# Cross attention of layer 0: weights transposed in blocks of 128 columns across the heads, values spread to fit

## The chip, the core and the metric

The kernel runs on one core of a Trainium2 chip. The core has five instruction queues that run side by side and meet at semaphores: TensorE for matrix products (PE in the profile, with its weight loads shown apart as PEld), VectorE (DVE), ScalarE (ACT), GpSimd (POOL) and SyncE (SP), which here only issues transfers. A queue runs its instructions in the order in which they were written: one that waits holds up all those behind it. The metric is the time of one execution on the device in microseconds; a result is the median over several runs.

## The reference, cut to what matters

The model is a two-layer decoder over x of shape [16, 256, 256], all in float32. Layer 0 has a linear attention, a cross attention to a context of 77 keys, and a mixture of 16 experts with two chosen per token; layer 1 has attention, a second cross attention and a quantized feed-forward block. The change touches the cross attention of layer 0 alone:

```python
q = jnp.einsum('bfd,dnh->bfnh', query_input, wq)      # 16 heads of 16
k = jnp.einsum('btd,dnh->btnh', source_input, wk)     # t: 77 keys
v = jnp.einsum('btd,dnh->btnh', source_input, wv)
q = q * HEAD_DIM ** (-0.5)
logits = jnp.einsum('btnh,bfnh->bnft', k, q) + bias
weights = jax.nn.softmax(logits, axis=-1)
attn = jnp.einsum('bnft,btnh->bfnh', weights, v)
return jnp.einsum('bfnh,nhd->bfd', attn, wo)
```

For each of the 16 batch entries and each of the 16 heads, 256 queries are weighted over 77 keys.

## The kernel before

The 4096 tokens are 32 tiles of 128 (`NT`), four tiles to a group (`NG` = 8), so that a group spans two batch entries. Each of the two stages that matter, `l0_attention` and `l0_cross`, is recorded whole before any of it is issued: `Plan` collects the operations, each with the tiles that it reads and writes, gives each a duration by fixed formulas (`Call`, L308), and then puts them in an order, always taking next the operation that can start first, or one that can start at most 150 ns later and stands earlier in the record. A copy (`nc.copy`, L112) may go to VectorE or to ScalarE, and the planner chooses. Because of the recorder, nearly all instructions of these stages carry the line L363, and the profile has to be read by the names of tiles.

`l0_cross` (L1009) walks over the tiles i = 0 to 31. For tile i it records the scores of tile i+1 ahead of the second half of tile i:

- `scores` (L1032): per half m of the heads (`KD` = 2 halves of 8 heads) two matmuls give `ps_sc`, 128 queries by 8 x 77 keys. VectorE adds the mask (`lx_s`), takes the maximum (`lx_mx`), GpSimd subtracts it, ScalarE takes the exponential, VectorE sums (`lx_sum`) and inverts (`lx_rec`), GpSimd widens the inverse (`lx_wide`).
- `weighted` (L1071): the weights `lx_s` [128 queries, 8 heads, 77 keys] are transposed to have the keys on the partitions. This is done head by head: eight transposes of 77 columns per half, four into each `ps_pt`, and two copies per half to `lx_sT` (77 x 512). Then 16 products `ps_rec` per tile multiply them with the values: each takes the 77 rows of one head and writes 32 rows, for a pair of heads, and two products (`par` 0 and 1) add up in the same place. That works since the values `lx_v` lie in a buffer [77, 16, 4, 16] of which the slots 1 and 2 stay zero, so that each head adds zeros to its neighbour's rows. ScalarE or VectorE copies the transposed inverse (`lx_rT`), VectorE multiplies (`lx_aT`), two products with `w_L_xattn_wo` follow in the same `ps_rec`, and VectorE adds the result to x.
- `cross_keys` (L943) and `cross_queries` (L981) prepare the group after the next: projections of keys, values and queries. The values of group g+2 go by one copy from `ps_v` into one of three `lx_v` buffers. The mask of the group is loaded by SyncE (`lx_bias`).
- the router of the experts (`l0_router`, L773): SyncE first fills `moe_x` with zeros (16 transfers of 640 KB), then, a group behind the attention, 64 scatters from GpSimd (`moe_x<-rh,slot`) write the token rows into it.

The groups 0 and 1 of keys, values and queries are prepared at the end of `l0_attention`, by `ahead` (L735).

The line that places the values before, and the loop of transposes:

```python
    nc.copy(
        X.vz[g % 3][:, :, ::3, :],
        ps[:S2].rearrange("p b (r h e) -> p (b r) h e", h=2, e=DH0),
    )
```

Of the kernel before, what the change touches and what calls it, by code (L numbers as in the profile page):

```python
# [18 lines left out]
F32 = mybir.dt.float32  # L19
# [8 lines left out]
P = 128  # L28
B, S, D = 16, 256, 256
S2 = 77  # L30
NT = B * S // P
NG = NT // 4
KD = D // P
H0 = 16
DH0 = 16
# [446 lines left out]
def matmul_k(E, ps, lhs, rhs):  # L482

    last = len(lhs) - 1
    for n, (a, b) in enumerate(zip(lhs, rhs, strict=True)):
        E.nc.tensor.matmul(ps, a, b, start=n == 0, stop=n == last)  # L486
# [33 lines left out]
def l0_attention(E, W, X, own):  # L520
# [9 lines left out]
    with ExitStack() as ctx, planned(E) as nc:  # L530
        c1 = ctx.enter_context(tc.tile_pool(name="la_c", bufs=1))
        wk = nc.ring(ctx.enter_context(tc.tile_pool(name="la_w", bufs=2)), 2)
        w3 = nc.ring(ctx.enter_context(tc.tile_pool(name="la_w3", bufs=3)), 3)
        pp = nc.ring(ctx.enter_context(tc.tile_pool(name="la_pp", bufs=2, space=PSUM)), 2)
# [194 lines left out]
        f = front(0)  # L729
# [3 lines left out]
        f = front(1)  # L733
        step(f)
        def ahead():  # L735

            cross_consts(E, W, X, own)
            yield
            for g in range(2):
                yield from cross_keys(E, W, X, g, own, pp)  # L740
                yield from cross_queries(E, W, X, g, wk, own, pp)

        for i in range(NT):
# [3 lines left out]
            if i == NT - 4:  # L747
                f = ahead()
# [12 lines left out]
            if a == 3:  # L761
                step(f)
                if i + 5 < NT:
                    f = front(i // 4 + 2)
# [156 lines left out]
def cross_consts(E, W, X, pool):  # L921

    nc = E.nc

    quarter = pool.tile([P, 2, 4], F32, name="lx_quarter")
    nc.gpsimd.memset(quarter, 1.0)
    nc.gpsimd.affine_select(
        quarter, quarter, [[-64, 2], [-16, 4]], ALU.is_ge, 0.0, base=0, channel_multiplier=1
    )
    nc.gpsimd.affine_select(  # L930
        quarter, quarter, [[64, 2], [16, 4]], ALU.is_ge, 0.0, base=15, channel_multiplier=-1
    )
    X.sel = pool.tile([P, 4], F32, name="lx_sel")
    nc.vector.tensor_tensor(X.sel, quarter[:, 0, :], quarter[:, 1, :], ALU.add)

    X.vz = [pool.tile([S2, 16, 4, DH0], F32, name=f"lx_v{n}") for n in range(2)]
    for t in X.vz:
        nc.gpsimd.memset(t, 0.0)  # L940


def cross_keys(E, W, X, g, own, pp):  # L943

    nc = E.nc
    cols = slice(2 * g * S2, (2 * g + 2) * S2)
    kd = []
    for m in range(KD):
        ps = pp.tile([P, 512], F32, name="ps_k", tag="pp")
        matmul_k(  # L950
            E, ps[:, : 2 * S2], [W.xk0[:, k, m * P : (m + 1) * P] for k in range(KD)],
            [W.ctxT[:, k, cols] for k in range(KD)],
        )
        src = ps[:, : 2 * S2].rearrange("p (b k) -> p b k", b=2)

        t = own.tile([P, 2, 4, S2], F32, name=f"lx_k{m}", tag=f"lx_k{m}")
        for n in range(4):
            if n % 2:
                nc.vector.tensor_scalar(
                    t[:, :, n, :], src, X.sel[:, n : n + 1], None, ALU.mult  # L960
                )
            else:
                nc.scalar.activation(t[:, :, n, :], src, AF.Copy, scale=X.sel[:, n : n + 1])
        kd.append(t)
    X.keyed[g] = kd
    yield
    ps = pp.tile([P, 2, D], F32, name="ps_v", tag="pp")
    for j in range(2):
        b = 2 * g + j
        matmul_k(  # L970
            E, ps[:S2, j, :], [W.ctxT[:, k, b * S2 : (b + 1) * S2] for k in range(KD)],
            [W.xv0[:, k, :] for k in range(KD)],
        )
    nc.copy(
        X.vz[g % 3][:, :, ::3, :],
        ps[:S2].rearrange("p b (r h e) -> p (b r) h e", h=2, e=DH0),
    )
    yield


# [28 lines left out]
def l0_cross(E, W, X, raw, made):  # L1009
# [9 lines left out]
    with ExitStack() as ctx, planned(E) as nc:  # L1019
        c1 = ctx.enter_context(tc.tile_pool(name="lx_c", bufs=1))  # L1020
        wk = nc.ring(ctx.enter_context(tc.tile_pool(name="lx_w", bufs=2)), 2)
        w3 = nc.ring(ctx.enter_context(tc.tile_pool(name="lx_w3", bufs=3)), 3)
        pp = nc.ring(ctx.enter_context(tc.tile_pool(name="lx_pp", bufs=3, space=PSUM)), 3)
        psc = nc.ring(ctx.enter_context(tc.tile_pool(name="lx_sc", bufs=2, space=PSUM)), 2)
        pm = nc.ring(ctx.enter_context(tc.tile_pool(name="lx_pm", bufs=1, space=PSUM)), 1)

        third = c1.tile([S2, 16, 4, DH0], F32, name="lx_v2")
        nc.gpsimd.memset(third, 0.0)
        X.vz.append(third)
        R = l0_router(E, W, c1, wk, w3, pp)  # L1030
# [40 lines left out]
        def weighted(i, held):  # L1071

            weights, wide = held
            vb = X.vz[i // 4 % 3]
            r0 = 8 * (i % 4 // 2)
            sT = {}
            for m in range(KD):
                for par in range(2):
                    pt = pp.tile([P, 512], F32, name="ps_pt", tag="pp")
                    for j in range(4):  # L1080
                        nc.tensor.transpose(
                            pt[:S2, j * P : (j + 1) * P], weights[m][:, 2 * j + par, :], E.ident
                        )
                    t = w3.tile([S2, 4, P], F32, name="lx_sT", tag="lx_sT", bufs=4)
                    nc.copy(t.rearrange("p n q -> p (n q)"), pt[:S2])
                    sT[m, par] = t
                yield


            pr = pm.tile([P, 512], F32, name="ps_rec", tag="pm")  # L1090
            for m in range(KD):
                nc.tensor.transpose(
                    pr[:, D + m * P : D + (m + 1) * P],
                    wide[:, 8 * m : 8 * m + 8, :].rearrange("p h e -> p (h e)"), E.ident,
                )
            with nc.together():
                for m in range(KD):
                    for par in range(2):
                        for j in range(4):
                            nc.tensor.matmul(  # L1100
                                pr[32 * j : 32 * j + 32, m * P : (m + 1) * P],
                                vb[:, r0 + 4 * m + j, 2 * par : 2 * par + 2, :].rearrange(
                                    "p r e -> p (r e)"
                                ),
                                sT[m, par][:, j, :], start=par == 0, stop=par == 1,
                                skip_group_check=True,
                            )
            rT = w3.tile([P, D], F32, name="lx_rT", tag="lx_rT", bufs=2)
            nc.copy(rT, pr[:, D:])
            aT = w3.tile([P, D], F32, name="lx_aT", tag="lx_aT", bufs=2)  # L1110
            nc.vector.tensor_tensor(aT, pr[:, :D], rT, ALU.mult)
            yield
            matmul_k(
                E, pr[:, D:], [aT[:, m * P : (m + 1) * P] for m in range(KD)],
                [W.xo0[:, m, :] for m in range(KD)],
            )
            nc.vector.tensor_tensor(E.xs[i], E.xs[i], pr[:, D:], ALU.add)
            yield

        none = iter(())  # L1120

        def step(side, n=1):
            for _ in range(n):
                next(side, None)

        held = scores(0)
        f = kv = route = last = none
        for i in range(NT):
            g, a = divmod(i, 4)
            mine = weighted(i, held)  # L1130
            if a == 0:
                step(route, 8)
                route = R.take(4 * g - 4) if g else none
                kv = cross_keys(E, W, X, g + 2, wk, pp) if g + 2 < NG else none
            if i + 1 < NT:
                held = scores(i + 1)
                mark = len(nc.ops) - 1
            if a == 1 or a == 2:
                step(f)
            step(route, 1 if g < NG - 1 else 3)  # L1140
            step(mine)
            if a == 0:
                step(f)
            else:
                step(kv)
            step(mine)
            step(route, 1 if g < NG - 1 else 3)
            step(mine)
            if a == 3 and i + 5 < NT:
                f = cross_queries(E, W, X, i // 4 + 2, wk, wk, pp)  # L1150
                step(f)
            step(mine)
            if g == NG - 1 and a:

                with nc.urgent(-80):
                    step(route, 8)
                    step(last, 8)
                    last = R.take(i - 1, 2) if a == 1 else R.take(i, 1, 0)
                    step(last, 3)
# [934 lines left out]
```

## Time and profile before

| | |
|---|---|
| median of 16 runs | 1738.24 us (1731.48 to 1742.69) |
| the profiled execution, its time | 1736.84 us |
| its span, first to last instruction | 1735.1 us |
| PE busy in the span | 1590.2 us (92%) |
| DVE busy | 1128.1 us (65%) |
| ACT busy | 733.7 us (42%) |
| POOL busy | 497.8 us (29%) |
| cross attention of layer 0, first scores to first product of the next stage's weights | from about 275 us to about 598 us |
| lx_s transposes, PE | 512 |
| copies ps_pt to lx_sT | 113 on ACT, 15 on DVE |
| ps_rec products with the values | 1024 passes (two for each of 512 products) |

The shares are averages over stages with different limits, so the stage of the change has to be read by itself. A piece that is listed as "x8" is a run of eight instructions in a row; the duration given there is that of the whole run. Matmuls are pipelined: eight transposes of `lx_s` in a row took 1.05 us (from 368.32 us on), while the mean of a single one is listed with 294 ns.

### The profile page before, as it was taken

What the parts mean: (1) busy time and instruction counts of PE and PEld (TensorE: products, weight loads), DVE (VectorE), ACT (ScalarE), POOL (GpSimd) and SP (SyncE); (2) the same over time, 40 slices, a digit from 0 to 9 for tenths busy, and PEclk for the clock granted to TensorE, in tenths of its full rate; (3) what the DMA queues carried; (4) which work ended last, traced back from release to release, by engine and by line L of the source; (5) the groups of instructions that cost most, each with busy time, mean ns of one, the idle gap of its engine ahead of it and who ended that gap; (6) DMA issues with size and microseconds to landing.
All of it is one profiled execution on the core that took longest, in us unless ns stands there. A gap on an engine that the chain in (4) does not pass through costs nothing.

```text
span 1735.1 us, 24227 instructions
## 1 busy us (share of the span) xinstructions
PE 1590.2 (92%) x9268; PEld 1067.3 (62%) x9268; DVE 1128.1 (65%) x2212; ACT 733.7 (42%) x1551; POOL 497.8 (29%) x570
## 2 busy tenths in 40 slices
PE   6999999999996789999997899999999789999799
PEld 3666666666664667777775665666666434433387
DVE  7988876999986343221123778866776643899941
ACT  4343324555553211111112555555555342667850
POOL 5332113565565300000003787433344100000000
PEclk9999999999997599999998999999999889999899
DMA  6000008110001154334322121000000000001111
GB/s 186 1 1 1 2 1 261 62 41 30 29 33 36 53 164 136 109 119 142 122 82 67 43 61 43 13 1 1 1 1 1 1 1 0 25 25 60 37 49 49
DMA packets 75231, 90.76 MB, mean 52 GB/s; under 512 B 11934, under 2 KB 64886, under 8 KB 75114
## 3 DMA queue, kind: packets, MB, share of 16 engines
q1 hardware_dynamic: 68970, 72.64, 13.1%
q0 software_dynamic: 6144, 16.57, 3.0%
q8 instruction: 73, 1.20, 0.3%
q14 instruction: 44, 0.36, 0.1%
HBM read 52.70 MB, written 36.70 MB: 52 GB/s over the span
## 4 chain that ended last, share of the span: by engine, by line
PE 65%; DVE 21%; issue 6%; ACT 4%; DMA 2%; POOL 1%; SPq 1%; another core or an unknown queue 0%; POOLq 0%; ACTq 0%; DVEq 0%
PE ps_y L363 7%; PE ps_h L363 7%; PE ps_pr L363 7%; PE ps_av L363 6%; PE ps_pt L363 5%; PE ps_sc L363 5%; PE ps_out L486 5%; PE ps_gate L486 5%; PE ps_rec L363 3%; PE ps_v L363 3%; PE ps_po L363 2%; DVE ff_g L1957 2%; DVE ff_ps L1828 2%; PE ps_ht L363 2%; DVE ff_pu L1828 1%
## 5 line engine op out<-in xcount | busy, mean ns | idle before, releaser
L363 DVE COPY ex_y<-ps_y 128x256 f32<-128x256 f32 x80 | 33.7, 424 | 217.1 <-PE ps_y L363 217.1
L363 POOL DMA_INDIRECT ex_yg<-moe_y,slot x64 | 63.1, 985 | 346.5 <-issue 345.0
L363 POOL TENSOR_TENSOR sa_e<-sa_e,sa_rec 128x1024 f32<-128x1024 f32 x64 | 121.7, 1908 | 127.4 <-PE ps_pt L363 68.9
L486 PE MATMUL ps_up<-ff_x,ffn_up 128*128 128x512 f32 x336 | 148.7, 601 | 7.1 <-DVE ff_pu L1828 4.3
L363 ACT ACTIVATE sa_e<-ps_sc,sa_top 128x256 f32<-128x256 f32 x256 | 118.0, 484 | 73.1 <-DVE sa_top L363 66.9
L363 PE MATMUL ps_y<-w,ex_h 128*128 128x256 f32 x640 | 141.5, 379 | 5.1 <-DVE ex_y L363 5.1
L363 PE MATMUL ps_h<-ex_xT,w 128*128 128x320 f32 x512 | 142.5, 436 | 0.5 <-ACT ex_h L363 0.5
L363 PEld LDWEIGHTS ps_y<-w,ex_h 128*128 128x128 f32 x640 | 121.4, 190 | 24.4 <-DVE ex_y L363 6.3
L363 ACT ACTIVATE ex_h<-ps_h 128x640 f32<-128x640 f32 x64 | 44.9, 703 | 187.0 <-PE ps_h L363 187.0
L363 PEld LDWEIGHTS ps_h<-ex_xT,w 128*128 128x128 f32 x512 | 96.0, 191 | 40.0 <-ACT ex_h L363 1.0
L486 PEld LDWEIGHTS ps_up<-ff_x,ffn_up 128*128 128x128 f32 x336 | 63.6, 192 | 92.1 <-issue 74.5
L486 PE MATMUL ps_out<-ffn_down,ff_g 128*128 128x256 f32 x384 | 85.9, 388 | 10.3 <-issue 10.3
L486 PE MATMUL ps_gate<-ff_x,ffn_gate 128*128 128x512 f32 x192 | 84.3, 602 | 6.7 <-DVE ff_x L1930 6.7
L486 PEld LDWEIGHTS ps_out<-ffn_down,ff_g 128*128 128x128 f32 x384 | 74.8, 195 | 21.8 <-issue 11.1
L363 DVE TENSOR_REDUCE sa_top<-ps_sc 128x4 f32<-128x1024 f32 x64 | 76.4, 1215 | 16.6 <-PE ps_sc L363 15.1
L363 POOL TENSOR_TENSOR lx_s<-lx_s,lx_mx 128x616 f32<-128x616 f32 x64 | 78.0, 1220 | 31.8 <-DVE lx_mx L363 24.7
L363 DVE TENSOR_TENSOR la_at<-ps_sc,la_tri 128x1024 f32<-128x1024 f32 x64 | 75.8, 1214 | 8.6 <-PE ps_sc L363 8.6
L363 PE MATMUL ps_pt<-ident,lx_s 128*77 128x128 f32 x512 | 77.2, 294 | 0.4 <-ACT lx_sT L363 0.3
L363 ACT COPY lx_sT<-ps_pt 77x512 f32<-77x512 f32 x113 | 61.8, 582 | 28.6 <-PE ps_pt L363 26.5
L363 POOL DMA_INDIRECT moe_x<-rh,slot x64 | 64.2, 1004 | 32.6 <-issue 12.4
L363 PE MATMUL ps_pt<-ident,sa_e 128*128 128x128 f32 x512 | 66.2, 279 | 7.3 <-DVE hT L363 2.3
L363 PEld LDWEIGHTS ps_pt<-ident,lx_s 128*77 128x77 f32 x512 | 63.7, 159 | 12.5 <-issue 5.1
(289 smaller groups left out, 3387.8 us busy)
## 6 DMA issues: line engine op xcount, KB each, us to landing
w<-in_L_ffn_w SPq DMA_DIRECT2D x32, 512.0 KB, 3.8
moe_x<-rt_zero SPq DMA_DIRECT2D x16, 640.0 KB, 8.7
ex_xg<-moe_x SPq DMA_DIRECT2D x15, 640.0 KB, 6.5
moe_y<-ex_y SPq DMA_DIRECT2D x15, 640.0 KB, 5.7
x<-in_x SPq DMA_DIRECT2D x32, 128.0 KB, 3.1
out_x<-x SPq DMA_DIRECT2D x32, 128.0 KB, 1.7
ff_u<-ff_c SPq DMA_DIRECT2D x6, 512.0 KB, 2.9
ff_c<-ff_u SPq DMA_DIRECT2D x6, 512.0 KB, 3.2
```

The source lines that it names most:

```text
L363: made = getattr(getattr(self.nc, self.engine), self.method)(*self.args, **self.kwargs)
L486: E.nc.tensor.matmul(ps, a, b, start=n == 0, stop=n == last)
L1828: E.nc.vector.tensor_reduce(out, in_, axis, ALU.max, apply_absolute_value=True)
L1957: nc.vector.scalar_tensor_tensor(gp, low16(gq, I16), sg16, low16(sig, U16), ALU.mult, ALU.mult)
```

## The change

The weights of one half are taken as one row of 8 x 77 = 616 columns and transposed in blocks of 128 columns, four whole ones and one of 104, without regard to where a head begins. Five transposes replace eight in each half, ten replace 16 in each tile. The four whole blocks of a half fill one `ps_pt` and one `lx_sT` [128, 4, 128]; the two blocks of 104, one from each half, share a third `ps_pt` and a new small tile `lx_sL`.

A pair of heads now lies on two neighbouring blocks: pair j (columns 154j to 154j+153) on the blocks j and j+1. So there are again 16 products per tile, two for each pair, but each over the 128 (or 104) rows of a block, with rows of other pairs meeting zeros. The values must lie accordingly: in a buffer `VALUES` = [128, 4 pairs, 2 parts, 2 batch entries, 2 halves, 32], where the 77 rows of a head stand at the partitions that its columns have in the block. For that the values are first copied to a buffer `lx_vs` (in the ring of `hT`), and 12 transfers per group, issued by SyncE, carry the 8 heads' rows from there into place; four of the eight heads cross a border between blocks and need two.

```diff
-    X.vz = [pool.tile([S2, 16, 4, DH0], F32, name=f"lx_v{n}") for n in range(2)]
+    X.vz = [pool.tile(VALUES, F32, name=f"lx_v{n}") for n in range(2)]
...
+VALUES = [P, 4, 2, 2, KD, 2 * DH0]
+BLOCKS = [(b, min(P, 8 * S2 - b * P)) for b in range(5)]
...
-def cross_keys(E, W, X, g, own, pp):
+def cross_keys(E, W, X, g, wk, own, pp):
...
-    nc.copy(
-        X.vz[g % 3][:, :, ::3, :],
-        ps[:S2].rearrange("p b (r h e) -> p (b r) h e", h=2, e=DH0),
-    )
+    v = wk.tile([P, KD, 512], F32, name="lx_vs", tag="hT")[:S2, 0, :]
+    nc.copy(v, ps[:S2].rearrange("p b d -> p (b d)"))
+    v = v.rearrange("p (b m h e) -> p b m h e", b=2, m=KD, e=DH0)
+    for h in range(8):
+        for b, rows in BLOCKS:
+            lo, hi = max(h * S2, b * P), min((h + 1) * S2, b * P + rows)
+            if lo < hi:
+                nc.sync.dma_start(
+                    X.vz[g % 3][
+                        lo - b * P : hi - b * P, h // 2, b - h // 2, :, :,
+                        h % 2 * DH0 : (h % 2 + 1) * DH0,
+                    ],
+                    v[lo - h * S2 : hi - h * S2, :, :, h, :],
+                )
...
-        third = c1.tile([S2, 16, 4, DH0], F32, name="lx_v2")
+        third = c1.tile(VALUES, F32, name="lx_v2")
...
-            r0 = 8 * (i % 4 // 2)
+            b = i % 4 // 2
...
+            def turn(m, blocks, pt, at):
+                flat = weights[m].rearrange("p h k -> p (h k)")
+                for n, (t, rows) in enumerate(blocks):
+                    nc.tensor.transpose(
+                        pt[:rows, (at + n) * P : (at + n + 1) * P],
+                        flat[:, t * P : t * P + rows], E.ident,
+                    )
+
             for m in range(KD):
-                for par in range(2):
+                pt = pp.tile([P, 512], F32, name="ps_pt", tag="pp")
+                turn(m, BLOCKS[:4], pt, 0)
+                t = w3.tile([P, 4, P], F32, name="lx_sT", tag="lx_sT", bufs=4)
+                nc.copy(t.rearrange("p n q -> p (n q)"), pt)
+                for n in range(4):
+                    sT[m, n] = t[:, n, :]
+                if m == 1:
+                    rows = BLOCKS[4][1]
                     pt = pp.tile([P, 512], F32, name="ps_pt", tag="pp")
-                    for j in range(4):
-                        nc.tensor.transpose(
-                            pt[:S2, j * P : (j + 1) * P], weights[m][:, 2 * j + par, :], E.ident
-                        )
-                    t = w3.tile([S2, 4, P], F32, name="lx_sT", tag="lx_sT", bufs=4)
-                    nc.copy(t.rearrange("p n q -> p (n q)"), pt[:S2])
-                    sT[m, par] = t
+                    for k in range(KD):
+                        turn(k, BLOCKS[4:], pt, k)
+                    t = w3.tile([P, KD, P], F32, name="lx_sL", tag="lx_sL", bufs=2)
+                    nc.copy(t[:rows].rearrange("p n q -> p (n q)"), pt[:rows, : KD * P])
+                    for k in range(KD):
+                        sT[k, 4] = t[:rows, k, :]
                 yield
...
-                    for par in range(2):
+                    for part in range(2):
                         for j in range(4):
+                            rows = BLOCKS[j + part][1]
                             nc.tensor.matmul(
                                 pr[32 * j : 32 * j + 32, m * P : (m + 1) * P],
-                                vb[:, r0 + 4 * m + j, 2 * par : 2 * par + 2, :].rearrange(
-                                    "p r e -> p (r e)"
-                                ),
-                                sT[m, par][:, j, :], start=par == 0, stop=par == 1,
-                                skip_group_check=True,
+                                vb[:rows, j, part, b, m, :], sT[m, j + part],
+                                start=part == 0, stop=part == 1, skip_group_check=True,
                             )
```

In `l0_cross` the call becomes `cross_keys(E, W, X, g + 2, wk, wk, pp)`, in `ahead` `cross_keys(E, W, X, g, wk, own, pp)`; nothing else differs.

## The prediction

> **What bounds the kernel now.** I read the busy times by stretch first, since the shares of the page mix stages. The columns: stretch, its length, then PE, PEld, DVE, ACT and POOL busy with counts, the granted clock, the transfers' share, GB/s.
>
> ```profile
> 288.40:315.20 26.80, 24.53 (x265) 18.68 (x263) 26.16 (x58) 17.20 (x34) 12.59 (x14) 1.00 0.83 273
> ...
> 390.10:427.30 37.20, 33.86 (x308) 24.17 (x308) 33.92 (x92) 20.69 (x42) 22.88 (x30) 1.00 0.11 34
> 427.30:464.50 37.20, 33.86 (x308) 24.16 (x308) 33.91 (x92) 20.68 (x42) 22.85 (x30) 1.00 0.11 34
> ...
> 513.00:597.60 84.60, 57.67 (x431) 43.29 (x430) 49.91 (x161) 29.32 (x57) 42.32 (x57) 0.71 0.13 45
> ```
>
> The cross attention has three parts: a start, a steady part in which four tiles take 37.2 us again and again, and from 513 us a tail, where nothing is full and the clock is 0.71. In the steady part two engines stand almost level: PE 33.86 us and DVE 33.92 us of 37.2. Relief of PE alone can therefore bring only what DVE still loses by waiting. So I looked next at what DVE waited for from 288 to 513 us (total, times, longest):
>
> ```profile
> DVE lx_aT L363 <- ACT lx_rT L363: 8.2, 14, 0.9
> DVE rhT L363 <- PE ps_rt L363: 1.2, 2, 0.8
> DVE lx_s L363 <- PE ps_sc L363: 1.1, 5, 0.2
> ```
>
> With two smaller ones (0.8 and 0.5) this is 11.8 us in 224.6 us, nearly all of it for work that comes out of PE. In the same stretch PE waited 15.7 us for DVE's `lx_aT`. Third, the chain of waits in one period (start, duration, piece):
>
> ```profile
> 411.94 1.29 PE ps_pt L363 x8
> ...
> 413.66 0.44 DVE lx_aT L363
> ...
> 436.37 0.58 DVE lx_sT L363
> ...
> 438.09 0.59 DVE lx_sT L363
> ```
>
> From 404.2 to 427 us the chain runs on PE, and DVE comes in for an `lx_aT` at a time; the period's end lies on DVE, with two copies of transposed weights in it. The pieces with `ps_pt` between 402.2 and 439.4 us add up to 0.46+0.87+1.29+0.66+0.33+1.00+0.50 = 5.1 us.
>
> **The change, part by part.** The durations, from the groups by form:
>
> ```profile
> L363 ACT COPY lx_sT<-ps_pt 77x512 f32<-77x512 f32 x113 | 61.8, 582 | 28.6 <-PE ps_pt L363 26.5 <-issue 2.0
> ...
> L363 ACT COPY sa_eT<-ps_pt 128x512 f32<-128x512 f32 x81 | 44.7, 611 | 14.5 <-PE ps_pt L363 11.8 <-PE ps_cs L363 2.0 <-issue 0.5
> ...
> L363 DVE COPY sa_eT<-ps_pt 128x512 f32<-128x512 f32 x47 | 30.0, 676 | 0.5 <-PE ps_pt L363 0.5
> ...
> L363 ACT COPY lx_rT<-ps_rec 128x256 f32<-128x256 f32 x32 | 11.9, 371 | 51.4 <-PE ps_rec L363 24.3 <-PE ps_pt L363 15.5 <-PE ps_sc L363 8.3
> ```
>
> *Transposes.* 16 per tile become 10. Eight of 77 columns in a row took 1.05 us, of which 0.27 is the last one's way through: (1.05-0.27)/7 = 0.111 us each. Sixteen of 128x128 (`sa_e`, layer 1) took 1.91 us: (1.91-0.28)/15 = 0.109. So width costs nothing and number does: 6 x 0.11 = 0.66 us a tile, 2.6 us a period, 21 us over 32 tiles of PE.
>
> *Products with the values.* 16 per tile as before; 32 passes over 77 rows took 1.01 us on the chain, and `ps_av<-la_at,la_v`, 128 rows and the same 32 columns, has a mean of 276 ns against 285. Nothing.
>
> *Copies.* The order in which the two built programs' instructions stand tells what the planner chose. Before: 113 `lx_sT` on ACT and 15 on DVE. After: 58 `lx_sT` and 22 `lx_sL` on ACT, 6 and 10 on DVE; one `lx_vs` and seven instead of three `rhT` go to DVE as well. ACT loses 113 x 0.582 - 58 x 0.611 - 22 x 0.371 = 22 us, and some more with `rhT`. DVE: 10 x 0.42 (256 wide, as its `ex_y` copies, 424 ns) + 6 x 0.676 + 0.67 + 4 x 0.69 = 11.7 us against 15 x 0.669 = 10.0. So DVE gets 1.7 us more in the stage, 0.2 to 0.3 us a period. But in the period that I compared, the two copies at its end are gone, and one of each kind stands in the middle instead.
>
> *What of it lies on the path.* At the most DVE stops waiting: 11.8 - 1.7 = 10.1 us. At the least nothing: PE's time goes into waits for DVE, 15.7 us now and more then. PE's part of the chain shrinks by 24/64 of 5.1 = 1.9 us a period, while DVE can give 11.8/6 = 2.0 less its 0.25, so 1.7; DVE should be the limit, with some waits left, since `lx_aT` still needs the last product, then a copy. I take two thirds, 6.5 us, and keep 0 and 10.1.
>
> *The start.* The first tile's transposes run at half clock (18 in 3.58 us, 0.2 each) on the chain; six fewer give 1.2 us; the copies behind them are fewer too, but the last product now waits for the small one. I take 1 us (0 to 1.2).
>
> *The tail.* On the chain from 515 to 585 us stand 0.89+1.03+0.26+0.90+0.23 us of `ps_pt` at full clock, 3.05 at half, then 4 x 1.81: 13.6 us. Six of sixteen gone would be 5.1 us. Against it: `ps_rec` now waits for the small copy, 0.37 us and the ways around it, in each of four tiles, and between the tiles the chain runs over DVE and POOL, where nothing changes. I take 3 us (-1 to 5.1).
>
> *Transfers.* 12 for each of 8 groups, of four pieces of 64 bytes per partition: 8 x 77 x 32 = 19712 packets. The page's hardware queue has 68970 packets in 13.1% of 16 engines' 1735 us, 53 ns each, at about 1 KB; at that price all of mine are 1.0 ms over 16 engines, 65 us of a stage of 320 us whose transfers fill 0.11 of the time in the steady part. They are covered: the values of group g+2 are written while group g runs, a whole period of 37 us ahead of their use, and a load of comparable smallness, `cx_bq`, landed after 4.3 us. For group 0 the copy was at 252.9 us and the first use at 286.8; twelve issues of 0.5 us and two rounds of 4.3 us end near 268. What SP has behind them: in `ahead` the loads for layer 1 (not used before 597 us), then two masks and the 16 zero fills of `moe_x` (277.9 to 304.3 us). Group 1's twelve come before most of those loads, group 2's among the zeros, where SP also waits for a copy (298.1 us before): 24 x 0.5 = 12 us later, landing by about 304 + 12 + 8.7 = 325 us. The first scatter was issued at 336.3 us; 11 us of cover, and POOL stalls beyond it.
>
> For how a transfer is spread, the Trainium skill (DMA: Bandwidth & Descriptors, Why a DMA increments its semaphore by 16 and not by 1) says that the number of engines is the largest up to 16 that divides the outermost sizes: 77 rows would go over 11 engines, 51 over 3, the single row over one. By that the 51 rows are 68 packets on each of three engines, an estimate of 3.6 us at 53 ns; it would change no term, and no run here shows it yet.
>
> *Sum.* 6.5 + 1 + 3 = 10.5 us off the span of 1735.1, so 1724.6; the profiled execution took 1736.84, 1.7 us around its span, and lies 1.4 us under the median of 1738.24. That makes 1727.7; I say 1728.
>
> **The rivals.** *DVE takes it all* (17%): PE is faster and waits. For it: DVE's 33.9 of 37.2 us and 1.7 us more of work. Against: its waits come from PE. Then the steady part gives 0 to 2, the tail as much: 1735 to 1739, say 1737.
>
> *PE loses its clock* (12%), the case on the slow side. One place in the trace shows it:
>
> ```profile
> 313.00:316.40 3.40, 1.06 (x16) 0.68 (x5) 3.23 (x10) 0.89 (x2) 1.39 (x3) 1.00 0.00 0
> 316.40:320.00 3.60, 3.60 (x15) 2.31 (x14) 2.93 (x6) 2.69 (x5) 2.24 (x3) 0.53 0.00 0
> ```
>
> After a wait of 2.33 us for `lx_aT` the clock was half for some 3.4 us. In the steady part it never was; the emptiest stretches there (374.4 to 377.8) have PE busy 2.43 of 3.40 us. In the new order one tile of each period has its `w_L_xattn_wo` products directly after the 16 products, where two score matmuls stood between, so PE waits there for copy and multiplication without cover, some 1.6 us and more if DVE is late. A half-clocked 3.4 us costs up to 1.7 us. Six such, one in each period, eat 10 us and give no change; two in each cost 20 - 10.5, so 1748. It decides from seven on.
>
> The skill (TensorE: Matmul & The Clock Gate, Why this matters for your kernels) asks for no PE gap over about 3 us. By that rule no gap here would cost the clock and the sum stays; the trace lost it after 2.33 us, and the trace decides.
>
> *Late zeros* (5%): were the fills to land 15 us after the first scatter is due, GpSimd's queue, with the subtractions behind, would stand still that long: 1728 + 15 = 1743.
>
> **How the numbers follow.** The forecast has 66%. Its own range is the sum of the lower bounds, 0+0-1, to that of the upper ones, 10.1+1.2+5.1: 1739 to 1722; the tail's clock (0.71 on the mean, half and full by turns) may shift by two spells of up to 1.7 us either way, so 1718 at the low end. To the high end I add part of the clock's case: 1742. 0.2% is 3.5 us, about what a measurement of this kernel can tell from no change: faster (under 1734.8) is the forecast, 0.66; no change is DVE's case, 0.17; slower is the clock and the zeros, 0.17.
>
> **What would show it.** Right: a period of 35 to 36.5 us; PE near 31.3 us in it, DVE near 34; DVE's waits for `lx_rT` down to some 4 us; no `lx_sT` copies on DVE at the period's end; zeros landed before the first scatter. Wrong: a period of 37 us or more with PE waiting for `lx_aT` over 20 us (DVE's case); spells of half clock between 320 and 513 us (the clock's); POOL waiting for SP's transfers at its first scatter; PE waiting for a transfer at `ps_rec`. A tail no shorter would take 3 us from the forecast.

## The result, and the profile after

The changed kernel takes 1756.07 us (median of 11 runs, 1751.34 to 1763.80) against 1737.66 us for the kernel before (1731.26 to 1742.69). The ratio is 1.0109, 95% interval [1.0096, 1.0122]: slower by 1.1%, some 19 us, where 10 us less were forecast. The profiled execution spans 1754.0 us against 1735.1.

| part of the profiled execution, us | before | after | forecast |
|---|---|---|---|
| first `lx_aT` after | 288.4 | 296.7 (+8.3) | -1 |
| steady part, first to 25th `lx_aT` | 213.2 | 225.2 (+12.0) | -6.5 |
| tail, to the next stage's weights | 95.8 | 94.9 (-0.9) | -3 |
| all behind it | 1137.7 | 1137.3 (-0.4) | 0 |

The busy times by stretch of the kernel after (start and end, length, then PE, PEld, DVE, ACT, POOL busy with counts, granted clock, transfers' share, GB/s); a line is four tiles, the last one the tail:

```profile
323.20:359.50 36.30, 32.37 (x284) 22.42 (x284) 33.09 (x90) 18.28 (x37) 22.10 (x28) 0.95 0.41 127
359.50:404.00 44.50, 36.51 (x288) 23.75 (x288) 37.49 (x97) 18.06 (x36) 24.75 (x32) 0.92 0.13 34
404.00:439.20 35.20, 32.03 (x282) 22.03 (x280) 32.73 (x93) 18.23 (x36) 21.76 (x28) 0.96 0.15 37
...
478.20:521.90 43.70, 33.35 (x284) 22.84 (x284) 35.76 (x96) 18.72 (x37) 25.02 (x32) 0.96 0.14 39
521.90:616.80 94.90, 64.28 (x480) 45.81 (x481) 62.55 (x195) 30.96 (x62) 47.61 (x68) 0.74 0.12 41
```

Before, a period was 37.1 to 37.5 us with 91 to 94 instructions on DVE. Now two are 35.2 and 36.3 us, as forecast, one is 39.0, and two are 44 us; the longest has 97 instructions on DVE, a shorter one 90: the planner's new order no longer repeats. No period has the full clock: seven spells of 3.4 us at half clock fall into the steady part, where there was one, at 316.4 us.

The border first. The waits of the kernel after from 262 to 297 us (total, times, longest), and SP's timeline (start, duration):

```profile
DVE ln_st L363 <- DMA lx_v<-lx_vs: 13.9, 1, 13.9
POOL lx_v L363 <- DMA lx_v<-lx_vs: 13.6, 1, 13.6
```
```profile
254.80 10.44 SPq L363 DMA_DIRECT2D lx_v<-lx_vs  x12
...
271.05 10.24 SPq L363 DMA_DIRECT2D lx_v<-lx_vs  x12
```

Twelve issues take 10.4 us, not 6. Nobody waits there for values: `ln_st` and the clearing of the third `lx_v` are first writes of the new stage that wait until group 1's transfers have read `lx_vs`, and SP issues the last of those at 281 us.

The steady part, the timeline of the kernel after around one stall (the bracket gives the idle time before and what ended it):

```profile
380.97 1.06 POOL L363 DMA_INDIRECT moe_x<-rh,slot  x1 [1.27 <-ACT lx_sT L363]
381.15 10.43 SPq L363 DMA_DIRECT2D lx_v<-lx_vs  x12
...
381.96 0.27 PE L363 MATMUL ps_rec<-lx_sL,lx_v 104*32 104x128 f32 x1
382.16 0.79 PE L363 MATMUL ps_sc<-lx_k,lx_q 64*128 64x308 f32 x4
...
382.88 0.77 PE L363 MATMUL ps_pt<-ident,lx_s 128*128 128x128 f32 x5
...
385.88 0.37 ACT L363 COPY lx_rT<-ps_rec 128x256 f32<-128x256 f32 x1 [4.68 <-remote]
...
386.76 2.07 PE L363 MATMUL ps_rec<-w_L_xattn_wo,lx_aT 128*128 128x256 f32 x4 [3.12 <-DVE lx_aT L363]
```

The last product ended at 382.23 us by its record, but ACT's copy behind it began at 385.88: PE's increment of the semaphore stands in the trace at 385.86, 3.6 us late, and those of the scores and transposes behind it follow within 0.12 us. DVE and then PE wait, and from 386.4 us PE runs at half clock. The same stands at 460.9 and 507.5 us. A semaphore is the counter by which one engine tells another that its work is done; I call this a late increment. "Remote" stands in the view where the profile names no instruction that ended the wait.

The terms of the copies came about as costed (611, 371 and 420 ns), in the groups by form:

```profile
L363 ACT COPY lx_sT<-ps_pt 128x512 f32<-128x512 f32 x58 | 33.6, 585 | 29.3 <-PE ps_pt L363 23.6 <-issue 4.1 <-remote 1.3
...
L363 ACT COPY lx_sL<-ps_pt 104x256 f32<-104x256 f32 x22 | 8.3, 376 | 1.8 <-PE ps_pt L363 1.6
...
L363 DVE COPY lx_sL<-ps_pt 104x256 f32<-104x256 f32 x10 | 4.2, 420 | 2.0 <-PE ps_pt L363 1.8
```

### The profile page after: what moved, and what is told of

It reads as the page before. It is cut to its first block, busy times and chain, and to the rows that moved or that the text cites. A ratio compares the mean times of both kernels' runs of the same rounds, so it can differ in the third digit from the quotient of the medians.

```text
span 1754.0 us, 23970 instructions
## 1 busy us (share of the span) xinstructions
PE 1583.9 (90%) x9076; PEld 1052.2 (60%) x9076; DVE 1130.2 (64%) x2218; ACT 714.2 (41%) x1513; POOL 498.7 (28%) x570
## 4 chain that ended last, share of the span: by engine, by line
PE 59%; DVE 24%; issue 7%; ACT 4%; POOL 3%; DMA 2%; SPq 1%; another core or an unknown queue 0%; POOLq 0%; DVEq 0%; ACTq 0%
PE ps_y L363 7%; PE ps_h L363 7%; PE ps_pr L363 7%; PE ps_av L363 5%; PE ps_out L486 5%; PE ps_gate L486 5%; PE ps_sc L363 4%; PE ps_pt L363 4%; PE ps_v L363 3%; PE ps_po L363 2%; DVE x L363 2%; DVE sa_top L363 2%; DVE ff_g L1985 2%; PE ps_rec L363 2%; DVE ff_ps L1856 2%
## 5 line engine op out<-in xcount | busy, mean ns | idle before, releaser
L486 PE MATMUL ps_out<-ffn_down,ff_g 128*128 128x256 f32 x384 | 85.9, 388 | 10.3 <-issue 10.3
L363 PE MATMUL ps_sc<-sa_latT,sa_q 64*128 64x256 f32 x512 | 69.7, 399 | 2.0 <-ACT sa_e L363 2.0
L363 PEld LDWEIGHTS ps_pt<-ident,sa_e 128*128 128x128 f32 x512 | 58.9, 145 | 18.2 <-DVE hT L363 4.0
L486 PEld LDWEIGHTS ps_gate<-ff_x,ffn_gate 128*128 128x128 f32 x192 | 37.0, 194 | 53.5 <-issue 52.7
```

The source lines that it names most:

```text
L363: made = getattr(getattr(self.nc, self.engine), self.method)(*self.args, **self.kwargs)
```

## The experiments

Chips differ. On two of them the kernel before takes 1721 to 1722 us, on the three others 1737 to 1742. Each of the five was used once, so that it is the chip, and not the occasion, is not shown. Times are therefore compared as ratios to the kernel before on the same chip, and parts within one chip wherever that is possible; which chip the two first profiles come from is not on record. "Late" says whether increments over 1.1 us late stand between 320 and 510 us; "half" is the time at half clock in the steady part.

| run | ratio [95%] | first lx_aT | steady | half | late |
|---|---|---|---|---|---|
| e1_no_transfers | 1.0017 [0.9998, 1.0035] | 288.0 | 221.2 | 20.5 | yes |
| e2_own_source | 1.0061 [1.0040, 1.0082] | 288.3 | 228.6 | 30.7 | yes |
| e3_only_01 | 1.0081 [1.0052, 1.0109] | 296.0 | 221.1 | 20.5 | yes |
| e4_before_plus | 1.0087 [1.0056, 1.0118] | 288.6 | 227.6 | 17.1 | yes |
| e5_six_more | 1.0083 [1.0055, 1.0110] | 288.4 | 214.6 | 3.4 | no |
| e6_later_end | 1.0064 [1.0037, 1.0091] | 287.8 | 210.6 | 10.2 | no |
| e7_border_later | 1.0035 [1.0020, 1.0050] | 289.5 | 210.0 | 10.2 | no |
| e8_no_scatters | 1.0006 [0.9994, 1.0019] | 289.9 | 211.2 | 17.1 | no |
| e9_later_2000 | 1.0079 [1.0064, 1.0094] | 291.4 | 229.7 | 30.7 | yes |
| e10_later_600 | 1.0053 [1.0037, 1.0069] | 288.0 | 223.0 | 21.2 | yes |
| e11_before_later | 1.0056 [1.0043, 1.0069] | 287.8 | 225.8 | 17.1 | yes |
| e12_before | 1.0001 [0.9991, 1.0011] | 288.2 | 212.8 | 0 | yes |
| f1_before | 0.9999 [0.9983, 1.0015] | 287.7 | 206.0 | 3.4 | no |
| f2_no_transfers | 1.0042 [1.0025, 1.0059] | 289.4 | 212.7 | 10.3 | no |
| f3_six_more | 1.0085 [1.0054, 1.0116] | 289.6 | 214.5 | 3.4 | no |
| f4_later_end | 1.0050 [1.0030, 1.0071] | 289.7 | 210.1 | 10.2 | no |
| f5_after | 1.0113 [1.0079, 1.0147] | 296.2 | 228.7 | 23.9 | yes |
| f6_after_no_scatters | 1.0004 [0.9992, 1.0015] | 296.1 | 211.1 | 17.1 | no |

e1 to e4, e5 to e8, e9 to e12, f1 to f4, and f5 with f6 each shared a chip.

### What the transfers cost (e1 to e4)

e1 leaves the transfers out when the planned order is issued, so that the order stays; e3 does it with `drop=g > 1`:

```diff
-                    v[lo - h * S2 : hi - h * S2, :, :, h, :],
+                    v[lo - h * S2 : hi - h * S2, :, :, h, :], drop=True,
...
-        made = getattr(getattr(self.nc, self.engine), self.method)(*self.args, **self.kwargs)
+        made = None if self.drop else getattr(getattr(self.nc, self.engine), self.method)(*self.args, **self.kwargs)
```

> The changed kernel in its own order of instructions, with all 96 transfers that place the values left out (the values stay zero, so the output is not the reference's). Theory A, the transfers cost the time, once at the border between the stages and again in every period: the first lx_aT comes near 288 us again, the steady part to the 25th lx_aT takes 205 to 214 us instead of 225.2, and the time is 1726 to 1732 us. Rival B, the new order of the products costs it by way of the clock: the border's 8 us come back and no more, the steady part stays at 222 to 226 us with its spells of half clock, and the time is near 1748 us.

> The changed kernel in its own order, with the transfers of the groups 0 and 1 kept and those of groups 2 to 7 left out (their values are then those of earlier groups or zero). Theory A: the border stays late by 8 us (first lx_aT near 297 us), the steady part takes 205 to 214 us, the time is 1734 to 1741 us. Rival B: steady part 222 to 226 us, the time stays at 1754 to 1758 us.

Ratios 1.0017 without any and 1.0081 with those of the groups 0 and 1. The border behaves as A says: 288.0 and 296.0 us. The steady part fell by only 4 us to 221, with six spells of half clock: nearer to B. So the transfers cost (1.0109 - 1.0017) of 1738 us, 16 us, of which 8.0 stand at the border (e3 against e1); the share of the steady part is read from e2. What is left after taking them out is no gain.

e2 gives group 1's `lx_vs` memory of its own:

```diff
-    v = wk.tile([P, KD, 512], F32, name="lx_vs", tag="hT")[:S2, 0, :]
+    if g == 1:
+        v = own.tile([P, 512], F32, name="lx_vs1")[:S2, :]
+    else:
+        v = wk.tile([P, KD, 512], F32, name="lx_vs", tag="hT")[:S2, 0, :]
...
-            wide = w3.tile([P, H0, DH0], F32, name="lx_wide", tag="lx_wide")
+            wide = w3.tile([P, H0, DH0], F32, name="lx_wide", tag="lx_wide", bufs=2)
```

> The changed kernel with the lx_vs of group 1 in memory of its own, so that no tile of the next stage lies where the transfers still read (lx_wide gets two buffers instead of three, to make room). Theory A1, the 8 us at the border are the next stage's first writes waiting for that memory: DVE's ln_st and GpSimd's lx_v no longer wait 13 us for lx_v<-lx_vs, the first lx_aT comes at 288 to 290 us, the time is 1746 to 1750 us. Rival, the border is late because the first products need group 0's values or because of the new order: the wait moves to another instruction there, the time stays at 1754 to 1758 us.

First `lx_aT` at 288.3 us: the 8 us at the border are the reused memory. DVE's wait for `lx_v<-lx_vs` fell from 13.9 to 6.9 us (group 0's transfers) and no longer decides:

```profile
DVE ln_st L363 <- DMA lx_v<-lx_vs: 6.9, 1, 6.9
```

The ratio is 1.0061. The steady part is 228.6 us, 7.4 us more than in e1, on the same chip and with the same order of instructions; with the border's 8.0 that is nearly all of the 16 us. In three places ACT's copy begins 3.6, 2.8 and 5.4 us after the end of the product that it reads, in e1, without transfers, 3.1, 2.1 and 2.6 us after it. One buffer of `lx_wide` less is an unlikely reason: f5 below has all three and 228.7 us.

e4 turns it round: twelve transfers of the same shapes in the kernel before, from `lx_v` to a spare tile, for the groups 2 to 7 (`lo`, `hi` and the loops as in the change):

```diff
+                    nc.sync.dma_start(
+                        X.spare[lo - b * P : hi - b * P, h, :, :, :],
+                        v[lo - h * S2 : hi - h * S2, :, :, h // 2, h % 2 * 3, :],
+                    )
```

> The kernel before with twelve transfers of the same shapes added for each of groups 2 to 7, from lx_v into a spare tile that nothing reads. Theory A: its steady part grows by 8 to 14 us, with ACT's lx_rT waiting 3 to 5 us while SP issues them, and the time is 1745 to 1752 us. Rival B: the transfers alone change nothing, 1735 to 1741 us.

1.0087: 15 us from transfers that nothing reads, with the old order (in the traces, instruction for instruction on PE, DVE, ACT and POOL) and the full work of PE. In each of the last four periods one increment is 3.4 to 3.5 us late, and `lx_rT` waits up to 4.3 us. A holds for this order.

### Whether gaps and the clock explain the rest (e5 to e8, again f1 to f4)

e5 repeats six of each tile's ten transposes; e6 changes one planner figure; e7 has all transfers, e2's memory (with two buffers of `lx_sum` and `lx_rec` in place of e2's `lx_wide`) and e6's figure:

```diff
-                    nc.tensor.transpose(
-                        pt[:rows, (at + n) * P : (at + n + 1) * P],
-                        flat[:, t * P : t * P + rows], E.ident,
-                    )
+                    for _ in range(2 if n < 3 and at == 0 and t < 3 else 1):
+                        nc.tensor.transpose(
+                            pt[:rows, (at + n) * P : (at + n + 1) * P],
+                            flat[:, t * P : t * P + rows], E.ident,
+                        )
```
```diff
             self.busy, self.tail = 2 * max(110, 0.84 * free(out)), 220
+            self.tail += 1000 if any("lx_v" in r[0] for r in self.reads) else 0
```

> The kernel without transfers, with six of the ten transposes of each tile done twice, so that PE has again 16 per tile. Theory C, the time that PE saved turned into gaps ahead of w_L_xattn_wo, and gaps that leave PE less than half busy over some 3.4 us halve its clock: in spite of 192 x 0.11 = 21 us more work on PE the half-clocked spells between 320 and 510 us fall from six to at most two, the steady part takes 210 to 217 us instead of 221.2, the time is 1734 to 1741 us. Rival D, the 128-row products, the copies or DVE's share of them cost the 8 us: the steady part stays at 221 us or grows to 234, the time is 1745 to 1758 us.

> The kernel without transfers, with nothing changed but one figure in the planner: it takes the products with the values to end 1000 ns later than it did, so that it puts other work of PE between them and w_L_xattn_wo. Theory C: at most two half-clocked spells between 320 and 510 us, PE's waits for lx_aT halved, steady part 207 to 214 us, 1731 to 1738 us. Rival D: steady part 219 to 223 us, 1743 to 1747 us.

> The changed kernel, all transfers in, with two edits: lx_vs of group 1 in memory of its own (lx_sum and lx_rec with two buffers instead of three, for room), and the planner's figure for the end of the products 1000 ns later. If both effects stand beside each other: first lx_aT at 288 to 289 us, steady part 3 to 6 us over that of the kernel without transfers and with the same order (210 to 219 us), 1734 to 1743 us. Rival D: steady part 225 us or more, 1747 to 1752 us.

> The kernel without transfers, with GpSimd's scatters moe_x<-rh of all groups but the first left out too. Theory E, the end of the products is told late while GpSimd issues scatters: ACT's waits of over 2 us for lx_rT between 320 and 510 us go, the gaps of PE with them, the steady part takes 207 to 214 us, the time is 1730 to 1738 us. Rival, the lateness has nothing to do with the scatters: ACT's lx_rT goes on waiting 2 to 3 us some three times, the steady part takes 219 to 223 us.

e8 leaves out, beside the transfers, the scatters of all groups but the first (`drop=i0 > 0`). The four steady parts (210.0 to 214.6 us) fall where C and E put them, and I read them so at first. But the ratios, 1.0083 and 1.0064 for e5 and e6, say slower than e1: this chip is one without late increments, the kernel before is faster on it too, and e8 can show nothing of theory E there. So e5 and e6 were run again with e1's kernel and the kernel before beside them:

> The kernel before, for its parts on the chip of the three others: ratio 1.000, steady part 208 to 214 us with at most one half-clocked spell.

> The changed kernel without its transfers, again: ratio 1.000 to 1.004. Theory C: its steady part is longer than that of the kernel before on this chip, or as long, with four half-clocked spells or more between 320 and 510 us. Rival D: it is longer with at most one spell.

> Six transposes of each tile done twice, 21 us more on PE. Theory C: at most two spells, and a steady part no longer than that of the kernel without transfers on this chip. Rival D: a steady part longer by 5 to 13 us, ratio 1.006 to 1.010.

> The planner's figure for the end of the products 1000 ns later, no transfers. Theory C: fewer spells than without the figure and a steady part shorter by 5 us or more. Rival D: no difference in the steady part beyond 2 us.

Now within one chip. The kernel before there, by stretch; two periods, then five (20 tiles):

```profile
387.40:422.80 35.40, 34.03 (x308) 24.12 (x308) 33.58 (x93) 21.28 (x41) 22.92 (x30) 1.00 0.11 36
422.80:458.20 35.40, 34.03 (x308) 24.11 (x308) 33.59 (x92) 21.28 (x41) 22.93 (x30) 1.00 0.11 36
...
314.50:493.80 179.30, 171.91 (x1544) 121.73 (x1544) 169.53 (x459) 106.21 (x205) 115.87 (x147) 0.99 0.10 34
```

The same columns for the changed kernel without its transfers (f2), and with six transposes repeated (f3):

```profile
352.30:393.00 40.70, 35.00 (x288) 22.75 (x288) 38.02 (x98) 18.18 (x36) 24.63 (x32) 0.96 0.10 34
393.00:428.00 35.00, 31.21 (x280) 21.25 (x280) 33.01 (x92) 18.02 (x36) 21.55 (x28) 1.00 0.10 32
...
315.90:502.10 186.20, 164.16 (x1420) 109.62 (x1420) 172.90 (x460) 91.05 (x181) 114.10 (x145) 0.97 0.10 32
```
```profile
315.90:504.10 188.20, 172.77 (x1540) 121.97 (x1540) 175.89 (x462) 92.62 (x181) 114.75 (x147) 0.99 0.10 33
```

In the kernel before DVE is busy 169.5 of 179.3 us: with DVE's work as it is, nothing PE does can bring more than the 9.8 it idles. Without the transfers PE is busy 7.8 us less, and DVE 3.4 us more and idle 3.5 us more (13.3): together the 6.9 us by which the 20 tiles are longer. f2 has the four spells that C asked for, two of them as one of 6.8 us that begins at the very end of the steady part, at 502.1 us. Then C falls: f3 has 3.4 us at half clock in the steady part instead of 10.3, and its steady part is 1.8 us longer than f2's, not shorter. The spells are there, but curing them with work brought nothing. This is not a test of the clock alone: the planner sees the repeated transposes too, and f3's order of instructions is another than f2's. f4, with the planner's figure, wins 2.6 us, half of what C asked, and its tail loses 2.4 (98.8 us against 96.4). D misses its figures as well (f2 has more than one spell, f3 is not 5 us longer, f4 differs by over 2). What stands is the sum above: on an engine that was full, DVE's added work and the idle time of the new order; which of order and copies makes how much was not taken apart.

### The planner's figure on the other kind of chip (e9 to e12)

The figure is set for the tiles 0 to 23 alone; e9 and e10 have all transfers and e7's memory, e11 is the kernel before with 1000:

```diff
+            nc.ops[-1].calls[-1].tail += 2000 if i < 24 else 0
```

> The changed kernel with all transfers, lx_vs of group 1 in memory of its own, and the planner's figure for the end of the products 2000 ns later for the tiles 0 to 23 alone, so that the tail keeps the changed kernel's order. If the cover ahead of w_L_xattn_wo is what the steady part lacks: no half-clocked spell between 320 and 500 us, steady part 205 to 211 us, tail 94 to 96, a ratio of 0.994 to 0.999 to the kernel before. Rival, DVE and the transfers hold the period by now: steady part 212 to 216 us, ratio 1.000 to 1.004.

> The same with 600 ns. The first theory expects a steady part between that of 1000 ns (210.0 us) and 214 us, and a ratio of 0.997 to 1.002; the rival the same as with 2000 ns.

> A control: the kernel before with the planner's figure 1000 ns later for the tiles 0 to 23. If the figure helps whatever the kernel, its steady part falls from 213 us to 206 to 210 us and the ratio is 0.995 to 0.999; if it helps only where PE has time left, the ratio is 1.000 to 1.004.

> The kernel before itself, for its parts on the same chip beside the three others: ratio 1.000, first lx_aT at 288 us, steady part 213 us, tail 96 us; the rest behind the stage is what differs from chip to chip, 1125 to 1140 us.

None of the three helps: 229.7, 223.0 and 225.8 us against 212.8, with increments 1.1 to 3.6 us late in other places. Other orders move them and don't avoid them. e12 gives 1.0001, so no difference comes from the comparison itself.

### What makes the increments late (f5, f6)

> The changed kernel itself. On a chip with late increments: first lx_aT at 297 us, steady part 225 us, lags of 2.7 to 3.7 us in four places between 320 and 510 us, ratio 1.011. On a chip without them: first lx_aT at 297 us, steady part 212 to 217 us, no lag over 1.1 us, ratio 1.007 to 1.011.

> The changed kernel, transfers in, with GpSimd's scatters moe_x<-rh of all groups but the first left out. Theory E (scatters make the increments late), on a chip with late increments: no lag over 1.1 us, steady part 211 to 217 us, ratio 1.001 to 1.005. Rival (SP's transfers make them late by themselves): lags of 2 us and more stay where SP issues the transfers, steady part 221 us or more. On a chip without late increments both expect the steady part of the changed kernel, within 3 us.

The chip was one with late increments, so the pair decides. f6 has e8's edit with the transfers kept. ACT's waits in the changed kernel from 296 to 525 us, and in the one without scatters:

```profile
ACT lx_rT L363 <- remote: 18.1, 4, 5.9
ACT lx_rT L363 <- PE ps_rec L363: 17.0, 17, 1.9
```
```profile
ACT lx_rT L363 <- PE ps_rec L363: 21.3, 22, 1.9
```

The steady parts of the two, columns as in the first table of stretches:

```profile
296.20:524.90 228.70, 192.22 (x1659) 129.65 (x1657) 197.54 (x515) 106.05 (x210) 127.13 (x159) 0.95 0.25 72
```
```profile
296.10:507.20 211.10, 187.22 (x1659) 127.35 (x1657) 196.48 (x515) 105.88 (x210) 95.03 (x128) 0.96 0.21 58
```

The "remote" waits are gone, and the steady part is 211.1 us instead of 228.7. In f5 there are three places in the steady part with increments over 2 us late (the first of each by 3.6, 2.7 and 5.3 us); in f6 none between 347 and 950 us is over 0.7, and the two that are left, 1.1 us late at 344 and 345 us, lie beside the first group's scatters, which f6 keeps. Theory E holds: GpSimd's scatters make PE's increments late. The transfers lengthen that where both run (e2 against e1), but do nothing of it alone. GpSimd is also 32 us less busy in f6, a rival for part of the 17.6 us, but a small one: on the two chips without late increments the steady part is 212.7 us with the scatters (f2) and 211.2 without them (e8), and the pairs e5 and f3, e6 and f4 agree there within 0.6 us. The ratio of 1.0004 is no gain: the work left out is missing on this side alone.

## Why the prediction was wrong

*Transposes, products, copies.* Right. A period has 24 instructions fewer on PE (308 to 284), products take 284 to 288 ns, the copies are as many as costed and within 26 ns as long.

*The steady part: the step that failed.* "At the most DVE stops waiting: 11.8 - 1.7 = 10.1 us", since its waits were "nearly all of it for work that comes out of PE". They were not for PE's work. The kernel before in the first profile, PE's timeline, then ACT's:

```profile
373.66 1.08 PE L363 MATMUL ps_rec<-lx_sT,lx_v 77*32 77x128 f32 x32
...
374.67 1.32 PE L363 MATMUL ps_pt<-ident,lx_s 128*77 128x128 f32 x10
```
```profile
376.08 0.37 ACT L363 COPY lx_rT<-ps_rec 128x256 f32<-128x256 f32 x1 [2.88 <-PE ps_pt L363]
```

And the same kernel on the chip of f1, the same two views:

```profile
372.98 1.08 PE L363 MATMUL ps_rec<-lx_sT,lx_v 77*32 77x128 f32 x32
```
```profile
374.13 0.37 ACT L363 COPY lx_rT<-ps_rec 128x256 f32<-128x256 f32 x1 [1.60 <-PE ps_rec L363]
```

The products end at 374.74 and the copy starts 1.34 us later; on f1's chip they end at 374.06 and it starts 0.07 us later. The first profile has eight such places of 1.2 to 1.3 us between 370 and 495 us, two in a period: more than enough for the difference between 213.2 and 206.0 us. On that chip the group of waits that carried my sum, 8.2 us, reads so:

```profile
DVE lx_aT L363 <- ACT lx_rT L363: 0.2, 1, 0.2
```

With four others, DVE's waits in that view come to 3.5 us, where I counted 11.8. A faster PE could not give back a wait that the scatters make. That they make it is shown by f6 for the new order; for the old one the times speak for it: all eight increments arrive 1.55 to 1.60 us after the start of a scatter's issue. The sign was there: a copy that waits 2.88 us for PE although the group it reads ended 1.34 us before. The chain that I added up has one too: the 1.29 us of `ps_pt` at 411.94 us in the prediction, a quarter of my 5.1, are a late increment: the products ended at 411.94 and their increment came at 413.24.

*Transfers.* "They are covered" failed twice. I priced when the values are needed, not what the transfers hold: `lx_vs` lies in a ring of the stage that ends, whose memory the next stage writes first (8.3 us, e2). And I looked at the share of the transfer engines, not at what SP's twelve issues do beside GpSimd's scatters (7.4 us by e2 against e1, some 14 us in the old order by e4, whose 227.6 us stand against 213.2 and 212.8 on other chips). An issue takes 0.83 us on the mean (96 of them), not 0.5; a transfer lands in some 2.1 us, not 4.3, and one of 51 rows in 2.2, where the sentences on the skill have an estimate of 3.6; the single row, which they give one engine, shows four increments behind the first.

*The start* would have been right within its bounds without the border's wait (-0.4 us in e1). *The tail* gained 0.9 us, within -1 to 5.1.

*The rivals.* "DVE takes it all" names the limit, and f1 shows it; it put its loss at nothing, where by f2 DVE got 3.4 us more work and 3.5 us more idle time in 20 tiles. "PE loses its clock" named what one sees, seven spells just where I put the point from which it decides; f3, without transfers and on another chip, speaks against its deciding, and no run shows what the spells cost in the changed kernel itself. The late zeros did not come: issued until 326.9 us, they had landed by 333.9, before the first scatter at 342.7.

Open: by what path scatters delay PE's increments, why some chips don't show it, and how the changed kernel with its transfers fares on such a chip, where it was not run. The best version with all the work in it, e7, is still slower than the kernel before, 1.0035 [1.0020, 1.0050]; none beats it.

## What to carry to other kernels

A wait that stands beside an engine's name is not yet that engine's work: set the start of the waiter against the end of the instruction that it reads, and take a gap of over a microsecond as a cost that a faster engine will not repay. For every transfer that is added, ask which memory it keeps busy and who writes there next, not only when its data is needed. And compare parts of profiles only within one chip: here the same stage of the same kernel takes 213 us in one profile and 206 in that of another chip.

## What the runs showed of the hardware

*Late increments.* In the two first profiles and on three of the five chips of the experiments PE's increments come 1.1 to 5.3 us late in places between 320 and 515 us. In the kernel before, in the first profile and in e12, there are eight such places each, and each increment arrives 1.5 to 1.6 us after the start of a scatter's issue. On the two other chips none is late, with the same instructions (f1 against the first profile).

*The clock.* I cut PE's time from 277 to 560 us of all 20 traces into the stretches of 3.41 us at whose borders the clock changes. Of 114 at full clock with PE busy under half, 111 were followed by half clock; of 1293 busier ones 16, and of 1203 busy over 65% none. The Trainium skill (TensorE: Matmul & The Clock Gate, Part 1: The HAM clock gate) describes such a free-running window of 3413 ns, and the lengths of the spells agree. It advises against gaps of over some 3 us (Why this matters for your kernels). Here less was enough, waits of 1.46 and 0.97 us in one stretch (350.1 to 353.5 us in e1), and the measurement decides.

*A transfer's engines.* The increments of one transfer agree with the rule of the skill that the prediction cites for the larger ones: behind a first increment, eleven for 77 rows (257.14 to 257.25 us, issued at 254.80), three for 51 rows (258.13 to 258.17 us, issued at 255.93). The single row has four (262.69 to 262.79 us, issued at 261.05). It landed in 1.6 to 2.4 us, little sooner than the others.

*DVE beside GpSimd.* `h<-x,ln_mv,ln_rstd` mostly takes 0.40 us on DVE; beside GpSimd's subtraction `lx_s<-lx_s,lx_mx` (1.23 us) three of them took 1.17, 1.79 and 2.26 us in f4, the last beside a scatter's issue as well. Such stretches are part of the 3.4 to 6.4 us that DVE is busier in f2 and f3 (`h` 10.0 and 13.1 us for 20, 9.3 in f1).
